# A four-layer graph kernel: the attention loop of its first layer in a written order, with a rational search step and zero rows for unused gather places

## The chip, the core and the metric

The kernel runs on one core of one Trainium2 chip. The metric is device time in microseconds (us) from the start to the end of one execution of the whole program. Five engines take part, each working through its own queue in order: TensorE (PE in the profile; its weight loads are PEld), VectorE (DVE), ScalarE (ACT), GpSimd (POOL) and SyncE (SP), which issues most DMA transfers. GpSimd issues the indirect ones, the gathers.

## What is computed

There are 4096 nodes with 256 features, one sparse 4096x4096 matrix `adj` (about 0.1% filled, and a diagonal), and four layers, each adding its output to `x` after a layer norm and a relu. Layer 0 is the expensive one. Cut to what matters:

```python
# layer 0, on h = relu(layernorm(x)); S = adj
R = S + eye;  R = R / R.sum(-1)
Xf = Xa = h;  Z = 0
for n in range(2):
    q = Xa @ W1.T @ W2.T;  k = Xa @ W3.T
    probs = softmax(q @ k.T)                  # 4096 x 4096
    # keep, in each row, the largest probabilities until 0.9 is reached
    A = probs * mask;  A = A / A.sum(-1)
    Xf = R @ Xf;  Xa = A @ Xa
    Z = Z + Xf @ U1[n].T + Xa @ U2[n].T
x = x + layernorm(h + Z) * ln_g + ln_b
# layer 1: tanh(R @ (h @ W) + b)      layer 2: graph attention with 4 heads
# layer 3: relu(adj @ (h @ W))
```

## The kernel before

**Two versions in one program.** `fast_layers` computes all four layers and counts rows in which one of its assumptions failed; only if that count isn't zero does `general_layers` compute everything again, with an exact search. In the profiled execution the fast version alone ran.

**Layer 0** is the function `layer0_step(n, ...)`, called for n = 0 and n = 1 and called step 0 and step 1 below. Each goes over 32 blocks of 128 rows. Before the loop it computes keys and queries and a guess of each row's largest logit (`minus_guess`). For a block b it then does this:

- `front(b)`: TensorE multiplies queries and keys (`pl`, L1008), ScalarE takes the exponentials into the 128x4096 tile `e` (L1011). Then comes a search for the threshold `t` below which a tenth of each row's sum lies. It has four rounds, two over the first 1024 columns and two over all 4096. In a round ScalarE passes over `e` twice with the current `t` as a bias, once with Sign and once with Relu (L1030); the pass writes a tile that nobody reads (`unread`), and its sum over the row is what counts. VectorE makes a new threshold of the two sums in a chain of operations on 128x1 columns (L1034 to L1054). In that chain GpSimd raises a ratio to a power (L1052). After the fourth round VectorE sets `hi`, an upper bound for the threshold (L1063, L1067).
- `diffuse(b)`: the product with the adjacency. In step 0 it is a full one: four transfers of 512 KB (`adj`), 33 matrix products into `pr` (L767), and VectorE marks which columns are used (`marks`, L1077, four reductions of 128x1024), and takes the reciprocal of the row sums (`rdeg`, L1080). In step 1 the used columns are known: GpSimd gathers up to 640 rows of the adjacency (`ac`) and of the values (`vg`) in five gathers each (L844), VectorE sets unused places of `ac` to zero (L1088), `ac` is written out for the later layers (L1094), and seven products follow (L859, L863). ScalarE scales the result (`xf`, L1099).
- `select(b)`: VectorE finds the exact threshold. One pass keeps what is below `hi` (`near`, L1110), 16 maxima of eight over it (`best`, L1115) and a list of the 48 largest (L1120, L1122) give the last kept value; a pass sets everything below it to zero in `e` (L1147), another removes surplus ties (L1150).
- `attend(b)`: 32 transposes on TensorE (`pat`, L1179), eight copies on ScalarE (`at`, L1181), 32 matrix products into `pa` (L1184), and a scaling (`xa`, L1186).
- `close(b)`, in step 1 only: transposes, eight products with the update weights (`pz`, L1198), a layer norm and the residual. The last four operations run on GpSimd (L737, L1215 to L1217).

**What sets the order.** The program is written for the tile framework. Its scheduler decides the order of each engine's queue from the order in the source, from its own estimate of durations, and from when buffers come free. The loop calls `front` two blocks ahead (`FRONTS = 2`, four buffers of `e`), so that the scheduler can fill one block's chain with another block's work.

**Between and after.** `list_columns` turns the marks of step 0 into lists of at most 160 columns for each quarter of the columns, cut into five index vectors of 128 (`column` for tables of values, `adj_row` for the adjacency). Unused places point at the first row of their quarter. Layers 1 to 3 use `ac` and these lists, with five gathers for each block.

Of the kernel before, what the change touches and what calls it, by code (L numbers as in the profile page):

```python
# [53 lines left out]
F32 = mybir.dt.float32  # L55
BF16 = mybir.dt.bfloat16
# [6 lines left out]
AX = mybir.AxisListType  # L63
PSUM = bass.MemoryType.PSUM
DRAM = bass.MemoryType.DRAM

P = 128
N = 4096
# [18 lines left out]
FRONTS = 2  # L87
# [558 lines left out]
def fast_layers(  # L646
# [47 lines left out]
    nc.gpsimd.memset(ones, 1.0)  # L694
    eights = const.tile([P, 8], F32, name="eights")
# [6 lines left out]
    for n in range(2):  # L702
        names = ("z", "t", "hi", "room", "full", "last", "extra")
        ends.append({k: const.tile([P, NB], F32, name=f"end_{k}{n}") for k in names})
# [6 lines left out]
    used = const.tile([P, CHUNKS, NB], F32, name="used")  # L711
# [5 lines left out]
    xf1_d = dram.tile([N, D], F32, name="xf1_d")  # L717
    xa1_d = dram.tile([N, D], F32, name="xa1_d")
    x1_d = dram.tile([N, D], F32, name="x1_d")
    q_d = dram.tile([P, N], F32, name="q_d")  # L720
    adjc_d = dram.tile([NB, P, CHUNKS + 1, P], F32, name="adjc_d")
    adj_rows = adjt.rearrange("b p c i -> (b p c) i")
# [54 lines left out]
    def list_columns(marks):  # L777

        with ExitStack() as st:
# [38 lines left out]
            nc.vector.tensor_scalar(used, at, 0.0, None, op0=ALU.is_gt)  # L818
            first = sb.tile([P, 1], F32, name="first")
            for q in range(QUARTERS):  # L820
                nc.vector.memset(first[q * 32 : (q + 1) * 32], q * float(N // QUARTERS))
            nc.vector.tensor_scalar(at, at, -1.0, 0.0, op0=ALU.add, op1=ALU.max)
            nc.vector.tensor_scalar(at, at, first, None, op0=ALU.add)
            nc.vector.tensor_copy(column, at)

            chunk_i = sb.tile([P, CHUNKS, NB], U32, name="chunk_i")
            nc.vector.tensor_scalar(chunk_i, column, 7, None, op0=ALU.logical_shift_right)
# [39 lines left out]
    def layer0_step(n, va, marks=None):  # L867

        with ExitStack() as st:
# [4 lines left out]
            tops = kt_pool.tile([P, NB, 1 + LIST], F32, name="tops")  # L874
            nc.gpsimd.memset(tops[:, :, 0:1], 0.0)
            end = ends[n]
# [86 lines left out]

            e_pool = st.enter_context(tc.tile_pool(name=f"e{n}", bufs=FRONTS + 2))
            adj_pool = st.enter_context(tc.tile_pool(name=f"adj{n}", bufs=3))
            sm = st.enter_context(tc.tile_pool(name=f"sm{n}", bufs=6))
# [5 lines left out]
            unread = one.tile([P, N], U8, name="unread")  # L972

            def small(name, width=1):
                return sm.tile([P, width], F32, name=name)

            def secant(power, old, new):

                diff, total = small("diff", 2), small("total", 2)
                for k in range(2):  # L980
# [551 lines left out]
```

## Time and profile before

| | |
|---|---|
| three runs | 4719.48, 4753.93, 4756.27 us; median 4753.93 us |
| the profiled execution | 4763.97 us, its span 4762.1 us |
| busy | PE 75%, DVE 59%, ACT 46%, POOL 28% of the span |
| up to the first logits of step 0 | 194 us |
| loop of step 0 | 194 to 1580 us |
| column lists, and what precedes the loop of step 1 | 1580 to 1787 us |
| loop of step 1 | 1787 to 3352 us |
| layers 1, 2, 3 | 390, 683 and 337 us |

The boundaries were read from the first and last instructions of each part. The share of busy time is an average over parts with different limits, so the loops are looked at one by one. A row of instruction groups gives the total busy time, the mean of one instruction in ns, and the idle time of the engine just before. In a line of the waits, the columns are the total in us, how often, and the longest. "granted clock" is the share of TensorE's full clock that it was allowed to run at.

### The profile page before, as it was taken

Reading aid. Unit: us, or ns where it says so; the run is one execution under the profiler, and the core shown is the slowest. Engines: PE = TensorE matmul, PEld = TensorE weight load, DVE = VectorE, ACT = ScalarE, POOL = GpSimd, SP = SyncE. Lnnn points to the kernel's source line nnn. Section 1 sums busy time; section 2 is a strip of 40 time slices with the busy share of each in tenths; the row PEclk is TensorE's granted clock in tenths of the full one; section 3 lists DMA queues with packets and bytes.
Section 4 is the critical chain, followed back from the end, with each engine's and each line's share of the span. In section 5 each row is a group of like instructions: output and inputs, shape, how many; then the busy total and the mean of one; then the engine's idle time right before and its main releaser. Section 6 shows DMA issues by size and latency. Waiting matters only on the chain.

```text
span 4762.1 us, 46890 instructions
## 1 busy us (share of the span) xinstructions
PE 3551.9 (75%) x14666; PEld 2659.7 (56%) x14666; DVE 2825.9 (59%) x9228; ACT 2188.1 (46%) x3157; POOL 1337.1 (28%) x1214
## 2 busy tenths in 40 slices
PE   4989899999999395878777878787455467777454
PEld 2566677677777253555555555555334356666333
DVE  2287887877888515676767676776211356666300
ACT  3377776666765016666666666664310320000300
POOL 0000010010010102444444444431046233231065
PEclk9799999999999677888888888898567765555767
DMA  2011121111112200111111111110235222221155
GB/s 74 28 55 57 53 62 56 48 61 62 53 51 65 72 26 29 42 37 44 37 44 36 45 36 45 35 32 14 85 101 165 92 80 65 68 67 39 66 166 160
DMA packets 160741, 292.11 MB, mean 61 GB/s; under 512 B 26466, under 2 KB 102626, under 8 KB 160482
## 3 DMA queue, kind: packets, MB, share of 16 engines
q1 hardware_dynamic: 124642, 193.94, 12.7%
q0 software_dynamic: 35840, 95.08, 6.7%
q8 instruction: 118, 1.93, 0.2%
q14 instruction: 141, 1.16, 0.1%
HBM read 242.65 MB, written 46.27 MB: 61 GB/s over the span
## 4 chain that ended last, share of the span: by engine, by line
DVE 27%; PE 24%; POOL 15%; issue 12%; ACT 11%; another core or an unknown queue 6%; DMA 3%; SPq 0%; DVEq 0%; POOLq 0%; ACTq 0%
ACT unread L1030 7%; POOL ratio L1052 6%; PE pa L1184 6%; PE acc L1424 5%; POOL vg L844 5%; DVE u L1410 3%; PE pv L1290 3%; DVE e L1147 2%; POOL ac L844 2%; DVE e L1150 2%; DVE best L1115 2%; PE acc L859 2%; DVE near L1110 2%; DMA ac<-in_adjt,adj_row 2%
## 5 line engine op out<-in xcount | busy, mean ns | idle before, releaser
L1030 ACT ACTIVATE unread<-e,t 128x4096 uint8<-128x4096 f32 (+1 forms) x384 | 1095.7, 2853 | 595.7 <-DVE t L1054 207.5
L1184 PE MATMUL pa<-xa,at 128*128 128x256 f32 x2048 | 619.5, 465 | 310.3 <-ACT at L1181 310.3
L1184 PEld LDWEIGHTS pa<-xa,at 128*128 128x128 f32 x2048 | 469.4, 236 | 479.4 <-ACT at L1181 395.7
L1052 POOL TENSOR_TENSOR ratio<-ratio,power 128x1 f32<-128x1 f32 x192 | 265.3, 1382 | 1086.1 <-DVE ratio L1048 610.8
L1184 PE MATMUL pa<-h,at 128*128 128x256 f32 x2048 | 509.8, 402 | 75.4 <-ACT at L1181 75.4
L1184 PEld LDWEIGHTS pa<-h,at 128*128 128x128 f32 x2048 | 395.8, 199 | 219.9 <-ACT at L1181 162.9
L767 PE MATMUL pr<-h,adj 128*128 128x257 f32 x2048 | 470.8, 384 | 13.4 <-ACT xf L1099 13.4
L1424 PE MATMUL acc<-tabg,u 128*128 128x65 f32 x1536 | 366.1, 418 | 145.4 <-DVE u L1418 139.1
L767 PEld LDWEIGHTS pr<-h,adj 128*128 128x128 f32 x2048 | 383.8, 191 | 103.5 <-issue 28.1
L1008 PE MATMUL pl<-kt,qb 64*128 64x512 f32 x1024 | 411.5, 665 | 39.5 <-ACT e L1011 39.5
L1424 PEld LDWEIGHTS acc<-tabg,u 128*128 128x128 f32 x1536 | 343.4, 329 | 173.8 <-DVE u L1418 161.4
L859 PE MATMUL acc<-vg,ac 128*128 128x256 f32 x768 | 240.4, 475 | 229.4 <-issue 77.9
L1181 ACT COPY at<-pat 128x512 f32<-128x512 f32 x512 | 284.0, 576 | 246.9 <-PE pat L1179 238.6
L844 POOL DMA_INDIRECT vg<-v_d,column x320 | 304.4, 951 | 315.1 <-DMA v_d<-v 167.2
L1115 DVE MAX8 best<-near 128x8 f32<-128x256 f32 x1024 | 372.7, 411 | 0.0
L844 POOL DMA_INDIRECT vg<-xf_d,column x160 | 268.6, 1679 | 307.5 <-PE pt L748 206.7
L859 PEld LDWEIGHTS acc<-vg,ac 128*128 128x128 f32 x768 | 178.5, 240 | 287.6 <-issue 85.4
L1011 ACT ACTIVATE e<-pl,minus_guess 128x1024 f32<-128x1024 f32 x256 | 284.2, 1117 | 117.1 <-DVE minus_guess L960 98.4
L1179 PE MATMUL pat<-ident,e 128*128 128x128 f32 x2048 | 276.3, 276 | 39.5 <-issue 24.8
L844 POOL DMA_INDIRECT tabg<-table_d,column x160 | 183.0, 1144 | 399.6 <-DVE rden L1432 269.3
L1179 PEld LDWEIGHTS pat<-ident,e 128*128 128x128 f32 x2048 | 241.5, 143 | 92.3 <-issue 55.4
L1110 DVE SCALAR_TENSOR_TENSOR near<-e,end_hi 128x4096 f32<-128x4096 f32 x64 | 286.9, 4483 | 1.0 <-DVE end_hi L1067 0.2
(486 smaller groups left out, 5205.0 us busy)
## 6 DMA issues: line engine op xcount, KB each, us to landing
adj<-in_adjt SPq DMA_DIRECT2D x128, 512.0 KB
ac<-adjc_d SPq DMA_DIRECT2D x96, 384.0 KB
adjc_d<-ac SPq DMA_DIRECT2D x32, 384.0 KB
v_d<-v SPq DMA_DIRECT2D x64, 128.0 KB
vg<-v_d SPq DMA_DIRECT2D x64, 128.0 KB
vg<-v_d,column POOLq DMA_INDIRECT x320
table_d<-tab SPq DMA_DIRECT2D x32, 132.0 KB
tabg<-table_d SPq DMA_DIRECT2D x32, 132.0 KB
```

The lines of the kernel that those rows point to most:

```text
L767: nc.tensor.matmul(acc, parts[c // CA][:, c % CA, :], v[:, c, :], start=(c == 0), stop=(c == NB - 1 and own is None),)
L844: nc.gpsimd.indirect_dma_start(out, None, rows, bass.IndirectOffsetOnAxis(ap=index, axis=0))
L859: nc.tensor.matmul(acc, ac[:, k, :], v[:, k, :], start=(k == 0), stop=(k == CHUNKS and not own))
L1008: nc.tensor.matmul(pl[:, r, :], qb[half], kt[half, j * 512 : (j + 1) * 512], start=True, stop=True)
L1011: nc.scalar.activation(e[:, j * 1024 : (j + 1) * 1024], pl.rearrange("p r c -> p (r c)"), AF.Exp, bias=minus_guess[:, b : b + 1], accum_ou ...
L1030: nc.scalar.activation(unread[:, :width], e[:, :width], func, bias=t, scale=-1.0, accum_out=to)
L1052: nc.gpsimd.tensor_tensor(ratio, ratio, power, op=ALU.pow)
L1110: nc.vector.scalar_tensor_tensor(near, e, hi, e, op0=ALU.is_lt, op1=ALU.mult, accum_out=low)
L1115: nc.vector.max(best[:, k, :], near[:, k * (N // SEG) : (k + 1) * (N // SEG)])
L1179: nc.tensor.transpose(pt[:, k, :], a[:, c * P : (c + 1) * P], ident)
L1184: nc.tensor.matmul(acc, at[:, k, :], va[:, c, :D], start=(c == 0), stop=(c == NB - 1))
L1424: nc.tensor.matmul(acc[:, h, :], u[:, k, h, :], tab[:, k, h * (DK + 1) : (h + 1) * (DK + 1)], start=(k == 0), stop=(k == CHUNKS),)
```

## The change

The change touches `fast_layers` alone.

1. The loop of `layer0_step` is cut into small functions, and `period(b)` writes out their order. It works on four blocks at a time: block b+2 gets its logits, exponentials and the two short rounds, b+1 the two long rounds and the bound, b is selected, and b-1 attended and closed. `tc.manual_schedule` makes VectorE, ScalarE and TensorE issue in just this order. The queues of GpSimd and SyncE stay the scheduler's.
2. In the search, `t * ratio ** power` gives way to a rational expression, computed on VectorE alone (`update`, `stepped`, and `bound` for the last round). A round has more column operations, and nothing on GpSimd.
3. Unused places in `column` now point at an added row N of each table, which holds zeros; so the multiplication of `ac` by `used` is dropped.
4. Smaller moves: h is stored (`h0_d`) and read back by block instead of computed again from x; the own rows of xf1 are read once more (`fb`); mean and variance of step 1 are taken in another way (`summed`, `spread`, `finish`), with the subtraction now on GpSimd; a GpSimd copy (`eighth`) takes the place of a VectorE reduction; four transposed pieces go through two copies instead of four; `adj` has four buffers in step 0 (before three), `ac` and `vg` two each in step 1 (before three).

```diff
+            def evaluate(b, k, funcs=(AF.Sign, AF.Relu)):
+                s = state[b]
+                width = PART if k < 2 else N
...
+                for func in funcs:
+                    nc.scalar.activation(
+                        unread[:, :width], s["e"][:, :width], func,
+                        bias=s["at"], scale=-1.0,
+                        accum_out=s["signs"] if func == AF.Sign else s["gap"],
+                    )
+            def measured(b, k):
...
+                nc.vector.tensor_scalar(twice, s["signs"], float(width), s["at"], op0=ALU.add, op1=ALU.mult)
+                nc.vector.scalar_tensor_tensor(
+                    low, twice, 0.5, s["gap"], op0=ALU.mult, op1=ALU.subtract
+                )
+                nc.vector.scalar_tensor_tensor(
+                    steep, s["gap"], -0.33 / 0.465, twice, op0=ALU.mult, op1=ALU.add
+                )
+                return low, steep, goal
+            def stepped(to, m, t):
+                den = small("den")
+                nc.vector.tensor_scalar(den, m, 0.5, 0.1, op0=ALU.add, op1=ALU.max)
+                nc.vector.tensor_scalar_min(den, den, 0.925)
+                nc.vector.reciprocal(den, den)
+                nc.vector.scalar_tensor_tensor(to, den, -1.0, t, op0=ALU.add, op1=ALU.mult)
+            def update(b, k):
...
+                low, steep, goal = measured(b, k)
+                den, num = small("step_den"), small("step_num")
+                nc.vector.scalar_tensor_tensor(den, low, goal, steep, op0=ALU.add, op1=ALU.mult)
+                nc.vector.scalar_tensor_tensor(num, low, goal, s["gap"], op0=ALU.subtract, op1=ALU.mult)
+                nc.vector.reciprocal(den, den)
+                m = small("m")
+                nc.vector.scalar_tensor_tensor(m, num, 0.5 / 0.465, den, op0=ALU.mult, op1=ALU.mult)
+                pair = small("next_pair", 2, 8)
+                stepped(pair[:, 0:1], m, s["at"])
...
-                    nc.gpsimd.tensor_tensor(ratio, ratio, power, op=ALU.pow)
...
+            def load(b):
+                s = state[b]
+                if n == 0:
+                    s["adj"] = load_adj(adj_pool, b)
+                    return
+                ac = s["ac"] = adj_pool.tile([P, CHUNKS + 1, P], F32, name="ac")
+                nc.sync.dma_start(ac[:, CHUNKS, :], adjt[b, :, b, :])
+                for k in range(CHUNKS):
+                    gather(ac[:, k, :], adj_rows, adj_row[:, k, b : b + 1])
+                nc.sync.dma_start(adjc_d[b], ac)
+                s["vg"] = gathered(adj_pool, xf1_d, b)
...
+            def diffused(b):
+                s = state[b]
+                if n == 0:
+                    nc.vector.reciprocal(rdeg[:, b : b + 1], s["pr"][:, D : D + 1])
+                s["xf"] = wk.tile([P, D], F32, name="xf", bufs=3)
+                nc.scalar.mul(s["xf"], s["pr"][:, :D], rdeg[:, b : b + 1])
...
+            def period(b):
+                old, cur, mid, new = (0 <= k < NB for k in (b - 1, b, b + 1, b + 2))
+                if n == 1 and 0 <= b - 2:
+                    finish(b - 2)
+                if cur:
+                    load(b)
+                if new:
+                    logits(b + 2, 0)
+                if mid:
+                    evaluate(b + 1, 2, (AF.Sign,))
+                if cur:
+                    below(b)
+                if n == 1 and cur:
+                    diffuse(b)
+                    diffused(b)
+                if old:
+                    flip(b - 1, 0)
+                    flip(b - 1, 1)
+                    take(b - 1, (0, 1))
+                    if n == 0:
+                        diffused(b - 1)
+                if mid:
+                    evaluate(b + 1, 2, (AF.Relu,))
+                    update(b + 1, 2)
+                if new:
+                    exponentials(b + 2)
+                if old:
+                    attend(b - 1, 0)
+                    attend(b - 1, 1)
+                    flip(b - 1, 2)
+                    flip(b - 1, 3)
+                    take(b - 1, (2, 3))
+                if new:
+                    logits(b + 2, 1)
+                    exponentials(b + 2)
+                    evaluate(b + 2, 0)
+                if cur:
+                    listing(b)
+                    if n == 0:
+                        mark(b, (0, 1))
+                if new:
+                    aim(b + 2)
+                    update(b + 2, 0)
+                if old:
+                    attend(b - 1, 2)
+                    attend(b - 1, 3)
+                    flip(b - 1, 4)
+                    flip(b - 1, 5)
+                    take(b - 1, (4, 5))
+                if mid:
+                    evaluate(b + 1, 3, (AF.Sign,))
+                if old:
+                    attend(b - 1, 4)
+                    attend(b - 1, 5)
+                    flip(b - 1, 6)
+                    flip(b - 1, 7)
+                    take(b - 1, (6, 7))
+                if mid:
+                    evaluate(b + 1, 3, (AF.Relu,))
+                if cur:
+                    decide(b)
+                    cut(b)
+                if mid:
+                    bound(b + 1)
+                if old:
+                    attend(b - 1, 6)
+                    attend(b - 1, 7)
+                    attended(b - 1)
+                    if n == 1:
+                        own_rows(b - 1)
+                        turn(b - 1, 0, state[b - 1]["fb"], va[:, b - 1, :D])
+                        turned(b - 1, 0)
+                if n == 0 and cur:
+                    diffuse(b)
+                    mark(b, (2, 3))
+                if new:
+                    evaluate(b + 2, 1)
+                    update(b + 2, 1)
+                if cur:
+                    drop(b)
+                if n == 1 and old:
+                    turn(b - 1, 1, state[b - 1]["xf"], state[b - 1]["xa"])
+                    turned(b - 1, 1)
+                    combine(b - 1)
+                    summed(b - 1)
+                    spread(b - 1)
+            with tc.manual_schedule(engines={ENGINES.DVE, ENGINES.Activation, ENGINES.PE}):
+                for b in range(-2, NB + 2 if n == 1 else NB + 1):
+                    period(b)
```

The new names stand for old work: `logits` is L1008, `exponentials` L1011, `evaluate` one round's Sign and Relu passes (rounds k = 0 to 3), `below` is L1110 and the 16 maxima, `listing` L1120 and L1122, `decide` L1126 to L1143, `cut` L1147, `drop` L1150 and the three operations after it, `flip` and `take` the transposes and copies of `attend`, each for 512 columns (group g of eight), `turn`, `turned` and `combine` the same for `close`. `bound` has 32 column operations, `update` 11 (12 for k = 2).

## The prediction

> **What bounds the kernel now.** I read the stages first: the share of busy time, stretch by stretch (us, then busy time and count of PE, PEld, DVE, ACT, POOL, then granted clock, DMA share, GB/s).
>
> ```profile
> 194.00:1580.00 1386.00, 1272.39 (x5696) 967.27 (x5696) 1109.34 (x3702) 935.81 (x1089) 120.64 (x132) 0.97 0.18 56
> 1787.00:3352.00 1565.00, 1193.67 (x4792) 861.02 (x4792) 1060.03 (x3787) 994.11 (x1311) 667.43 (x547) 0.87 0.12 38
> ```
>
> In step 0 TensorE is nearly full; in step 1 no engine is, so waits set the pace. `near` (L1110) starts at 234.9 and last at 1525.4 in step 0, at 1830.1 and 3293.0 in step 1: 41.6 and 47.2 us a block. Then the waits:
>
> ```profile
> POOL ratio L1052 <- DVE ratio L1048: 641.3, 89, 16.4
> ACT unread L1030 <- DVE t L1054: 207.5, 88, 11.6
> ACT unread L1030 <- DVE end_z L1019: 194.2, 28, 7.6
> ACT xf L1099 <- DVE rdeg L1080: 26.9, 17, 2.1
> ```
>
> ScalarE waits for thresholds that pass through GpSimd. The last line, small now, matters below: only a reciprocal of `pr` stands before `xf`. The trace in order of time shows why GpSimd is slow, and what a dependent VectorE operation costs:
>
> ```profile
> 854.35 0.25 DVE L1132 TENSOR_SCALAR out__6135<-ahead_of,end_room 128x48 f32<-128x48 f32 x1
> 854.63 0.21 DVE L1134 SCALAR_TENSOR_TENSOR kept<-out__6135,tops 128x48 f32<-128x48 f32 x1
> 854.87 0.20 DVE L1136 TENSOR_REDUCE end_t<-kept 128x1 f32<-128x48 f32 x1
> ...
> 2306.92 4.49 DVE L1110 SCALAR_TENSOR_TENSOR near<-e,end_hi 128x4096 f32<-128x4096 f32 x1
> ...
> 2307.03 4.78 POOL L1052 TENSOR_TENSOR ratio<-ratio,power 128x1 f32<-128x1 f32 x1 [1.48 <-DVE power L1045]
> ```
>
> A power beside `near` lasts 4.78 us, otherwise 0.55. Each of the first three operations starts 0.03 us after its predecessor ends. The large groups (busy total, mean ns, idle before):
>
> ```profile
> L1030 ACT ACTIVATE unread<-e,t 128x4096 uint8<-128x4096 f32 x256 | 948.8, 3706 | 290.1 <-DVE t L1054 153.2 <-DVE ra L1153 95.2 <-issue 30.6
> L1147 DVE SCALAR_TENSOR_TENSOR e<-e,end_t 128x4096 f32<-128x4096 f32 x64 | 286.6, 4477 | 0.0
> L1150 DVE MATCH_REPLACE8 e<-drop,e 128x4096 f32<-128x4096 f32 x64 | 282.2, 4409 | 0.0
> ```
>
> TensorE's pieces, run together:
>
> ```profile
> 801.50 3.73 PE L1184 MATMUL pa<-h,at 128*128 128x256 f32 x16
> 805.06 1.03 PE L1179 MATMUL pat<-ident,e 128*128 128x128 f32 x8
> 819.33 14.18 PE L767 MATMUL pr<-h,adj 128*128 128x257 f32 x64
> ```
>
> **The change, part by part.** VectorE, per block: `below` 4.52 and 16 maxima starting 0.327 apart, 9.8; `listing`, five rounds of 0.717 and a last maximum, 3.9; `decide` 1.8; `cut` 4.5; `drop` 4.4 and three columns, 4.9; marks 4 x 1.13. The column operations last 0.145 to 0.21 (L1034 to L1067), and in a written chain each waits for the last: `update`, 11, is 1.8 by that spacing, `bound`, 32, 4.8. The nearest extremes are 0.07 each, if all ran independently (0.8 and 2.2), and 0.24 (2.6 and 7.7). I take 1.8 and 4.8, since nearly all are dependent. With `aim` 0.3, VectorE needs 40 in step 0, 36 in step 1 (no marks, `summed` 0.6).
>
> *Step 0.* Let `below(b)` start at 0. ScalarE did the long Sign pass during the preceding `drop`, copies two pieces by 4, and next in its queue is `xf(b-1)`. Its `rdeg` stands behind `below(b)` in VectorE's queue, although `pr` is ready: 9.95. That is a new wait of 6, and behind it on ScalarE are the long Relu pass and everything after. Adding ScalarE's rows: `xf` to 10.3, Relu 3.8 to 14.1, two exponentials at 1.10, two copies 0.95, two exponentials to 19.4, two short passes at 1.24 to 21.8, two copies to 22.8, Sign 3.7, copies 1.2 with a short wait to 27.7, Relu to 31.5. `bound(b+1)` on VectorE waits for that (it was free at 30.0): to 36.3; marks 2.3, `update` 1.75, `drop` 4.9: 45.2. VectorE has waited 4.15 + 1.4.
>
> TensorE is done with the first two groups at 8.2; its next item, the second half of the logits, waits for `pl`, which the exponentials free at 15.3: idle for 7.2. What such a gap costs shows in stretches of 3.4 us (granted clock third from the end):
>
> ```profile
> 2149.10:2152.50 3.40, 0.06 (x1) 0.00 (x0) 0.56 (x2) 3.40 (x3) 2.20 (x4) 1.00 0.07 19
> 2152.50:2155.90 3.40, 2.42 (x6) 1.95 (x7) 1.67 (x11) 3.40 (x7) 2.91 (x4) 0.51 0.24 66
> 2155.90:2159.30 3.40, 3.40 (x10) 2.64 (x9) 1.23 (x8) 1.89 (x5) 2.44 (x3) 0.50 0.31 93
> 2159.30:2162.70 3.40, 3.40 (x17) 2.28 (x16) 1.11 (x5) 2.13 (x4) 0.56 (x1) 0.99 0.10 33
> ```
>
> One empty stretch, then 6.8 at half clock: up to 3.4 us lost, and 0 if the slow part falls into the gap. The groups that follow (3.7 of products, 1.0 of transposes) are on the path, since ScalarE's copies wait for them with no slack. Most of the slow part falls after the gap, so I take 2.5: 47.7 a block, 6.1 more than now. Times 31: +189.
>
> The Trainium skill ("TensorE: Matmul & The Clock Gate", Part 1) says that half rate ends after one busy window of about 3.4 us. By that alone the loss would be 1.7, step 0 +164 and the kernel 4670; this trace shows two windows.
>
> *Step 1.* There is no `rdeg`. ScalarE waits at 0 for `summed`, then `spread` 0.6, Sign 3.7, `xf` 0.4 (seven products, done at 3.4), copies 1, Relu 3.7, exponentials 2.2, copies 0.95, exponentials 2.2, short passes 2.4, copies 0.95, Sign 3.7, copies 1.2, Relu 3.8: 26.8. Then `bound` 4.8, `update` 1.75, `drop` 4.9, `summed` 0.6: 38.9. TensorE's gaps are under 2.8 each, so I add 0.3 for its clock: 39.2 against 47.2, times 31: -248.
>
> *At nothing:* the removed powers (265.3 us of L1052) and L1088 (0.83 x 32, on VectorE's path before) are inside these sums. `eighth` on GpSimd, between 0.15 and 4.8 with a wait like the power's, is needed only at the end. The subtraction on GpSimd (between 0.35, L741 on VectorE, and 1.4) hides beside VectorE's maxima; uncovered it costs only the tail. `h0_d`, 4 MB, is about 19 by the wait for x at the start, hidden by what precedes the loop. SyncE gets two more 128 KB reads a block; behind its write of `ac`, which waits for the gathers, stand `qb` and these, all with two buffers, so a block early. The gathers' number is unchanged; some 160 of 640 places are unused (128 rows at 0.1% hit about 480 columns) and now read one row instead of four: between 0 and +32 (TensorE's 31.6 us of waits for gathers in layers 1 and 3, doubled); I take 0. Filling and draining the loops stays at about 40 and 55 us: 0, +-15.
>
> **Sum:** 4764.0 + 189 - 248 = 4705 against the profiled execution; the median of the runs is 10 lower: 4695.
>
> **The rivals.** *Step 0 stays warm:* if the slow clock falls into the gap, 45.2 a block, +112: 4620. For it: the gap is twice the empty stretch. Against: the slow part above lasted 6.8.
>
> *The scheduler still places `rdeg` early,* so that the written order isn't what the queue gets, or the columns overlap more: step 0 at VectorE's 40 to 41.6: 4460 to 4510. For it: the wait was at most 2.1 us before. Against: `rdeg` is on an ordered engine.
>
> *Slower: gathers late in step 1.* `diffuse(b)` now stands ahead of block b-1's transposes in TensorE's queue, and these feed the whole ScalarE chain. Slack is 0.9; each us beyond costs 32. The kernel gets slower than now by 1% from 4.2 us on. If GpSimd issues block b's gathers in its own period, after `finish` (at 8) and at 1.25 each, they end at 20.5, 17 late: 5210. For it: one queue in order, two buffers instead of three, and GpSimd waited 206.7 us for a buffer of `vg`. Against: that buffer is now freed by `diffuse(b-2)`, so the gathers can run a period ahead. A few us late: 4850.
>
> *The rational step misses,* and `general_layers` runs: 28 passes like L1110 for 64 blocks alone are 8030 us. Against: both forms share goal and bounds.
>
> **How the numbers follow.** Forecast 0.50, between 4640 and 4760; warm clock 0.17; early `rdeg` 0.10; late gathers 0.20; miss 0.03. The range 4530 to 4850 leaves out half of the early case and most of the late ones. About 1% (48 us) is what a measurement of this kernel can tell from no change; below 4706 lie 0.29 of the forecast and the two gains, 0.56; within 1% 0.21 and 0.02 of late gathers, 0.23; slower 0.21.
>
> **What would show it.** In step 0: `near` 47.7 apart (13 or 14 of the stretches), "ACT xf <- DVE rdeg" the largest new wait at about 6 x 31 us, TensorE idle 7 us before the second logits and half clock after it. In step 1: `near` 39.2 apart, VectorE over 90% busy, no wait of `pr` for gathers. I am wrong if step 0 gets faster, or if step 1 gains less than 5 us a block.

## The result, and the profile after

The changed kernel took 4902.6 us in the median (four runs, 4883 to 4921) against 4755.1 for the kernel before, run beside it: a ratio of 1.033, 95% interval 1.027 to 1.040. It is slower by 3%; 4695 was forecast. The profiled execution took 4921.4 us, its span 4919.2. Here and below a time is the median of all runs, and a ratio compares only those in the faster of two states that the runs of a kernel show.

First the two loops, as in the first view of before: one stretch for each, us, then busy time and count of PE, PEld, DVE, ACT, POOL, granted clock, DMA share, GB/s.

```profile
235.00:1704.00 1469.00, 1194.00 (x5390) 923.98 (x5391) 1175.24 (x3792) 893.06 (x1028) 6.45 (x31) 0.89 0.16 51
2007.00:3454.00 1447.00, 1061.40 (x4494) 795.14 (x4495) 1058.94 (x3756) 930.34 (x1149) 507.95 (x466) 0.85 0.15 44
```

Step 0 was near the forecast and step 1 was not: `near` starts 47.4 us apart in step 0 (41.6 before, 47.7 forecast) and 46.7 in step 1 (47.2 before, 39.2 forecast). In the steady part both loops have the same period, 47.78 us, which is 14 of the 3.41 us stretches of the clock. Everything outside the two loops kept its length.

The waits, in us in total, times, and the longest:

```profile
DVE next_pair L1068 <- ACT unread L1038: 286.7, 61, 7.0
...
PE pr L872 <- DVE h L1346: 144.6, 30, 6.6
...
ACT xf L1304 <- DVE full_goal L1089: 138.6, 21, 6.6
...
ACT at L1249 <- remote: 133.6, 28, 5.4
...
ACT xf L1304 <- DVE rdeg L1302: 69.2, 10, 8.6
```

GpSimd's wait for a ratio (641.3 us before) is gone. The two lines of `xf` together, 208 us in 31 blocks, are the forecast wait for `rdeg` (a small operation that starts at the same time is sometimes named in its place). The line "at <- remote" was not forecast: ScalarE waits 4.8 us in each of 28 blocks, and no operation of another engine ends when that wait ends ("remote": the profile names no operation that ended it).

One period of step 0, in order of time, with the wait before each in brackets:

```profile
895.95 4.48 DVE L1156 SCALAR_TENSOR_TENSOR near<-e,end_hi 128x4096 f32<-128x4096 f32 x1
...
898.30 1.07 ACT L1249 COPY at<-pat 128x512 f32<-128x512 f32 x2 [3.27 <-PE pat L1242]
...
905.78 0.15 DVE L1302 RECIPROCAL rdeg<-pr 128x1 f32<-128x1 f32 x1
905.96 0.47 ACT L1304 ACTIVATE xf<-pr,rdeg 128x256 f32<-128x256 f32 x1 [6.59 <-DVE rdeg L1302]
906.34 3.70 ACT L1038 ACTIVATE unread<-e,next_pair 128x4096 uint8<-128x4096 f32 x1
...
910.16 0.16 DVE L1068 SCALAR_TENSOR_TENSOR pair<-twice,gap 128x1 f32<-128x1 f32 x1 [4.05 <-ACT unread L1038]
...
911.27 3.78 PE L1010 MATMUL pl<-kt,qb 64*128 64x512 f32 x8 [7.73 <-ACT e L1022]
914.98 4.53 PE L1258 MATMUL pa<-h,at 128*128 128x256 f32 x16
```

This is the forecast chain: the reciprocal starts 9.8 us after `near`, because it stands behind the maxima; `xf` waits 6.6 for it; the long pass and VectorE's update follow late; and TensorE, idle for 7.7, runs its next pieces at half clock (it has gone cold, as it is called below).

The same view of one period of step 1, where `near` started at 2796.80:

```profile
2813.68 1.04 PE L1242 MATMUL pat<-ident,e 128*128 128x128 f32 x8
...
2814.39 0.19 ACT L1038 ACTIVATION_READ_ACCUMULATOR unread<-e,ones 128x1 f32 x1
...
2816.46 0.96 POOL L857 DMA_INDIRECT vg<-xf_d,column  x1 [0.30 <-issue]
...
2819.31 1.07 ACT L1249 COPY at<-pat 128x512 f32<-128x512 f32 x2 [4.73 <-remote]
...
2819.95 4.63 PE L1258 MATMUL pa<-xa,at 128*128 128x256 f32 x10 [5.23 <-ACT at L1249]
```

The eight transposes end at 2814.7 and ScalarE is free from 2814.6, but its copy of them starts at 2819.3. An engine tells the others by a signal (the update of a semaphore) that an operation is done. The trace's records of signals show what ScalarE waited for: TensorE's signal for these transposes arrives at 2819.29, 4.6 us after their end. In between GpSimd is sending off the last of ten gathers. TensorE stands idle for 5.2 us by then and goes on at half clock.

### The profile page after: what moved, and what is told of

Its sections match the earlier page's. It is cut to its first block, busy times and chain, and to the rows that moved or that the text cites. A ratio compares the mean times of both kernels' runs of the same rounds, so it can differ in the third digit from the quotient of the medians.

```text
span 4919.2 us, 47246 instructions
## 1 busy us (share of the span) xinstructions
PE 3462.0 (70%) x14666; PEld 2645.9 (54%) x14666; DVE 2970.5 (60%) x9617; ACT 2176.2 (44%) x3061; POOL 1081.9 (22%) x1057
## 5 line engine op out<-in xcount | busy, mean ns | idle before, releaser
L1038 ACT ACTIVATE unread<-e,next_pair 128x4096 uint8<-128x4096 f32 (+1 forms) x384 | 1097.2, 2857 | 226.6 <-DVE next_pair L1082 220.5
L1258 PE MATMUL pa<-xa,at 128*128 128x256 f32 x2048 | 542.4, 424 | 165.5 <-ACT at L1249 165.5
L1258 PEld LDWEIGHTS pa<-xa,at 128*128 128x128 f32 x2048 | 426.1, 214 | 275.9 <-ACT at L1249 209.4
L1010 PE MATMUL pl<-kt,qb 64*128 64x512 f32 x1024 | 329.9, 765 | 333.4 <-ACT e L1022 315.4
L775 PE MATMUL pr<-h,adj 128*128 128x257 f32 x2048 | 450.5, 379 | 0.0
L1010 PEld LDWEIGHTS pl<-kt,qb 64*128 64x128 f32 x1024 | 105.3, 224 | 471.1 <-ACT e L1022 360.6
L1162 POOL COPY eighth<-best 128x16 f32<-128x16 f32 x64 | 13.5, 211 | 1545.3 <-DVE full_goal L1089 1068.2
L1161 DVE MAX8 best<-near 128x8 f32<-128x256 f32 x1024 | 340.9, 411 | 6.3
L1365 POOL TENSOR_TENSOR scale<-var,minus_half 128x1 f32<-128x1 f32 x32 | 143.2, 4474 | 853.7 <-DVE var L1363 853.7
L1202 DVE SCALAR_TENSOR_TENSOR e<-e,end_t 128x4096 f32<-128x4096 f32 x64 | 286.6, 4478 | 0.0
```

Source lines behind the costliest of these rows:

```text
L775: nc.tensor.matmul(acc, parts[c // CA][:, c % CA, :], v[:, c, :], start=(c == 0), stop=(c == NB - 1 and own is None),)
L1010: nc.tensor.matmul(pl[:, r, :], s["qb"][rows], kt[rows, j * 512 : (j + 1) * 512], start=True, stop=True,)
L1038: nc.scalar.activation(unread[:, :width], s["e"][:, :width], func, bias=s["at"], scale=-1.0, accum_out=s["signs"] if func == AF.Sign else ...
L1161: nc.vector.max(best[:, k, :], near[:, k * (N // SEG) : (k + 1) * (N // SEG)])
L1202: nc.vector.scalar_tensor_tensor(s["e"], s["e"], last, s["e"], op0=ALU.is_ge, op1=ALU.mult, accum_out=s["held"])
L1258: nc.tensor.matmul(s["pa"], s["at", g][:, k, :], va[:, c, :D], start=(c == 0), stop=(c == NB - 1))
```

## The experiments

I held four theories. A: step 0 is slow because `xf` on ScalarE waits for `rdeg`, which stands behind `below` on VectorE. B: ten gathers in one go hold back TensorE's signals in step 1. C (added after the first runs): whether signals are late depends on the chip or the run, and not on the code. D: what is left above 39.2 in step 1 is TensorE's slow clock after its wait for `summed`. A last group takes the change apart. The runs came on five occasions, each on another chip, with the kernel before beside them on the same chip; ratios are to that.

**The reciprocal moved.**

```
                     take(b - 1, (0, 1))
-                    if n == 0:
-                        diffused(b - 1)
...
                     take(b - 1, (4, 5))
+                    if n == 0:
+                        diffused(b - 1)
```

> After's kernel with one move in step 0: the reciprocal of the row sums and the scaling of block b-1 (diffused) come behind the copies of pieces 4 and 5, not behind those of 0 and 1. Theory A (step 0 is 47.8 us a block because ScalarE waits for a reciprocal that stands behind `below` on VectorE): the waits of xf for rdeg, full_goal and the like in step 0 (234 us) go, near starts 42 to 43 us apart there instead of 47.4, the kernel is 130 to 170 us shorter, about 4750. Rival (TensorE's slow clock after its gap locks step 0 to 14 stretches of 3.41 us, whatever ScalarE waits for): under 40 us, above 4860.

4512.6 us, ratio 0.965 (0.960 to 0.970). Step 0:

```profile
240.00:1564.00 1324.00, 1164.41 (x5383) 919.26 (x5384) 1175.09 (x3791) 882.38 (x1028) 6.42 (x31) 0.95 0.18 56
```

Its VectorE does the same 1175 us of work, in 1324 us and not in 1469, at a granted clock of 0.95 and not 0.89: 42.7 us a block. Theory A holds: the place of the reciprocal, and of the scaling that waits for it (both were moved), costs 145 us. But the kernel gained more than that, because step 1, whose code is as in after, ran at 40.5 us a block. Three other kernels ran on the same chip:

**Fewer gathers, or later ones.**

```
-            gather(v[:, k, :], v_d, column[:, k, b : b + 1])
+            nc.sync.dma_start(v[:, k, :], v_d[k * P : (k + 1) * P, :])      (vg plain, step 1's loop)
...
-                    gather(ac[:, k, :], adj_rows, adj_row[:, k, b : b + 1])
+                    nc.sync.dma_start(ac[:, k, :], adjt[b, :, k, :])        (ac plain)
...
                     below(b)
+                if n == 1 and 0 <= b - 2:
+                    finish(b - 2)                                            (finish behind below)
```

> After's kernel, but in the loop of step 1 the rows vg are read by five plain reads of fixed rows on SyncE's queue instead of five gathers on GpSimd's (so the diffusion there adds the wrong rows; the same bytes). Theory B (ten gathers in one go hold back the signals that TensorE sends, 4.6 us for the copies of pieces 4 and 5, and TensorE goes cold by it): the 133.6 us of ScalarE's remote waits go, near is 40 to 42 us apart in step 1 instead of 46.7, the kernel about 4700 to 4750. Rival B2 (the five gathers of adjacency rows, or the write of the 384 KB of ac, hold the signal): the remote waits stay near 4.7 us a block and the time within 40 us of 4902. Rival B3 (the signal was only the first of several waits of the same length, so another takes its place, the slow clock above all): the remote waits go and the time falls by less than 60 us.

> After's kernel, but in the loop of step 1 the adjacency rows ac are read by five plain reads of fixed chunks on SyncE's queue instead of five gathers (so the diffusion there multiplies wrong weights; the same bytes). The gathers of vg then run from 8 to 14.5 us after near instead of from 14.5 to 20.6. Theory B (ten in one go hold the signal): the remote waits go or shrink under 2 us a block, 4700 to 4760. If five gathers of 1 KB rows are enough to hold a signal, it is held earlier in the period, at the copies of pieces 2 and 3, and the time stays above 4830.

> After's kernel with finish(b-2) emitted behind below(b): VectorE starts near without the wait for the spread on ScalarE (0.73 and 0.15 us a block), and on GpSimd the ten gathers of block b come ahead of finish(b-2), so about 6 us later in the period before or at its start. Theory B: the held signal moves with the gathers to another hand-over, between 4 us a block worse and, if it falls into ScalarE's long passes, 5 us a block better: 4700 to 5030, with the late deliveries ending where the gathers end. Rival (the hold belongs to pieces 4 and 5 or to the write of ac, not to the gathers): late deliveries stay at the copies of pieces 4 and 5, and the time falls by 25 to 30 us for the wait on the spread alone.

4656.3, 4653.7 and 4642.3 us, ratios 0.993 (0.989 to 0.996), 0.995 (0.992 to 0.999) and 0.992 (0.989 to 0.995). Step 1 had 40.5 us a block in all three and none of the waits "remote". Taken alone the two kernels with plain reads would have looked like a proof of theory B. They are none: the kernel with the moved reciprocal kept all ten gathers and had 40.5 too.

**After and before once more.** So after was run with nothing changed on another chip, and before on two.

> After's kernel with nothing changed, run once more, since the four runs above all showed step 1 at 41.0 us a block, the one in which step 1's code is the same as after's too. Theory C (late signals of TensorE during gathers depend on the chip or the run, and step 1 of after is 41.0 us a block wherever they are on time): either late deliveries are counted in hundreds and step 1 is near 46.7, ratio 1.033, or there are a handful and step 1 is near 40.5, between the loops 285 to 288 us and not 303, ratio 0.992 to 0.998. Rival (the code of step 0 decides by the phase in which step 1 is entered): few late deliveries, but step 1 at 46.7 all the same.

> The kernel before with nothing changed, for its profile where signals of TensorE come on time (or not). If late signals cost it something too, its step 0 and step 1 stay near 41.6 and 47.2 us a block, and the 72 us by which it was faster there (4683 and 4687 against 4755) lie between the loops and in the layers behind them. If step 1 too was slowed by them, it shows below 46.

> The kernel before, for its profile. On a chip with signals on time: the 70 us by which it is faster there than on the others lie between the loops (some 15, as for after) and behind the loops (40 to 95, as for after), and its two loops stay at 1290 and 1464 us. If its second loop is shorter by more than 30 us, late signals cost before something in step 1 as well.

After took 4656.0 us there, ratio 0.994 (0.991 to 0.998), with this in its two loops:

```profile
236.00:1704.00 1468.00, 1195.20 (x5389) 926.01 (x5390) 1174.67 (x3789) 892.79 (x1028) 6.41 (x31) 0.89 0.16 51
1992.00:3249.00 1257.00, 1007.29 (x4494) 757.26 (x4495) 1061.83 (x3755) 926.57 (x1149) 505.96 (x466) 0.91 0.17 51
```

Step 0 is the same to a microsecond; step 1 is 190 us shorter with the same operations on every engine. The place shown above, in this run:

```profile
2533.56 1.04 PE L1242 MATMUL pat<-ident,e 128*128 128x128 f32 x8
...
2534.27 0.19 ACT L1038 ACTIVATION_READ_ACCUMULATOR unread<-e,ones 128x1 f32 x1
2534.36 1.05 ACT L1249 COPY at<-pat 128x512 f32<-128x512 f32 x2
...
2534.98 3.72 PE L1258 MATMUL pa<-xa,at 128*128 128x256 f32 x16 [0.38 <-ACT at L1249]
```

The copy starts as soon as ScalarE is free, and TensorE stays warm. I counted as late TensorE's signals that arrive over 0.6 us after the modelled end of the last matmul before them, and measured the parts of each profiled run from the starts of `near`:

| run | late signals | start to loop | step 0 | between | step 1 | behind |
|---|---|---|---|---|---|---|
| before, first | 175 | 234.9 | 1290.5 | 304.8 | 1462.8 | 1469.1 |
| before, third occasion | 163 | 235.3 | 1287.6 | 303.5 | 1464.1 | 1464.5 |
| before, fifth occasion | 3 | 231.8 | 1286.0 | 293.1 | 1464.9 | 1365.4 |
| after, first | 222 | 235.7 | 1468.7 | 303.3 | 1446.5 | 1465.1 |
| after, second occasion | 3 | 236.0 | 1468.5 | 287.9 | 1256.6 | 1370.3 |

Theory C holds as far as that it isn't the code alone: the same kernel has three late signals on one occasion and some 170 or more on another. All profiled runs of an occasion were of the same kind. Since each chip was used on one occasion, chip and occasion can't be told apart; "a chip with late signals" is short for both. Before has none in its loops on either kind, so both loops take the same time; nearly all its late ones lie in the sparse layers behind, which are about 100 us longer in these profiled executions. In the medians it loses some 70 (4751 and 4755 against 4682 to 4687). After loses much the same there, and 190 us more in step 1, where 56 signals are late.

**Is it the ten gathers?** Theory B could only be tested on a chip with late signals, and the chip can't be chosen.

```
-    s["vg"] = gathered(adj_pool, xf1_d, b)            (in load; load a period ahead)
...
+    held = small("held_seen")
+    nc.gpsimd.tensor_copy(held, state[b]["held"])     (waits for cut(b))
+    state[b + 1]["vg"] = gathered(adj_pool, xf1_d, b + 1)
...
+    with tc.manual_schedule(engines={..., ENGINES.Pool}):
```

> The kernel with plain reads of vg in step 1's loop once more (the diffusion there adds the wrong rows). Where after's own run beside it has late deliveries: Theory B (ten gathers in one go hold the signals) has near at 41.0 in step 1 and none late there; rival B2 (the other gathers or the write of ac) has 46.7 and about 2 late ones a block. Where after's own run has none, both are 41.0.

> After's kernel with the ten gathers of a block in two bursts of five: those of adjacency rows behind finish, those of vg behind a 128x1 copy on GpSimd that waits for what cut gives, some 10 us later; the same bytes, the same gathers, all results as before. Theory B (where a chip delivers late, it is ten gathers in one go that hold TensorE's signals, until 2.9 us after the last of them starts): no late signals in step 1's loop, its period 41 us and not 46.7, ratio 0.99 to 1.00 on a chip with late signals (counts near 170 from the sparse layers behind remain). Rival (the write of ac, or any gather at all): late ones stay, at another hand-over, and the period is above 44. On a chip with signals on time: 41.0 in any case.

> The kernel with plain reads of ac in step 1 once more (the diffusion there multiplies wrong weights), five gathers a block instead of ten. On a chip with late signals: Theory B has no late signals in step 1's loop and 41 us a block; if gathers of 1 KB rows alone are enough, late ones of up to 4 us stay and the period is above 44.

> After's kernel with the ten gathers in two bursts of five, once more. On a chip with late signals: Theory B has none late in step 1's loop and a period of 41 us; the rival (any gather, or the write of ac) has late ones at another hand-over and above 44. On a chip with signals on time 41.0 and nothing learned on this.

All four had their signals on time and 40.5 us a block (4623.0, 4626.4, 4622.5 and 4621.9 us); they decide nothing on B. What speaks for B comes from the runs on the other kind. In after all 56 late signals of step 1 arrive 2.78 to 3.03 us after the issue of the last of ten gathers. In the kernel with the power put back (below) the median of 55 is 2.81. In a kernel with finish behind below (the third of the next group) the gathers end 4 us earlier in the period, and the median of 60 late signals is again 2.90 after the last one; they are late by only 1.25 us there and cost little. Once their loops are steady, before sends at most five gathers at a time and the kernel without the written order at most six, and no signal is late there. The latter kernel begins step 1 with 15 gathers in a row, and three signals are late just behind these.

The layers behind the loops tell one rival off. In the first run of after 79 of the 222 late signals lie in layer 1, 82 in layer 3, and none in layer 2. Layers 1 and 3 gather rows of values alone, mostly in runs of 10 to 45 at a time, and write no `ac`; layer 2 gathers five at a time for most of its length, and none of its 90 signals is late. The other five runs with late signals show the same. So neither the gathers of adjacency rows nor the write of `ac` is needed for late signals, and long runs of gathers go with them. It is still a pattern and not a test: in layers 1 and 3 some signals are late behind five gathers only, 10 us after a longer run, and the two runs with the bursts taken apart met no late signals.

**Both moves, and what is left of step 1.** The first kernel has the reciprocal behind `update(b + 1, 2)`, the scaling behind the second exponentials, and finish behind below; the second also has step 1's gathers and diffusion product a period ahead, the product in TensorE's gap, and `z` in a buffer of the transposes; the third has the moves and fills that gap:

```
+                if n == 1 and cur and mid:
+                    diffuse(b + 1)                                       (second)
                 if n == 1 and old:
                     turn(b - 1, 1, ...)
...
                     logits(b + 2, 0)
+                if n == 1 and old:
+                    idle = ps.tile([P, 4, P], F32, name="pat", tag="pmisc")
+                    for k in range(28):
+                        nc.tensor.transpose(idle[:, k % 4, :], ident, ident)   (third)
```

> After's kernel with both moves: in step 0 the reciprocal on VectorE behind update(b+1, 2) and the scaling on ScalarE behind the second exponentials, where neither waits; in step 1 finish(b-2) behind below(b). If signals are on time: step 0 from 42.9 to about 41.5 us a block, as the 1.2 us that xf still waited and half of VectorE's 2.55 us go; step 1 41.0 as before; about 4470 where the kernel before is 4683, ratio 0.955. If signals are late during gathers: step 0 the same, step 1 between 41 and 47.8.

> The kernel of both moves, and in step 1 the gathers of block b+1 asked for a period ahead, its diffusion product put into TensorE's gap before the second turn of block b-1, and z in a buffer of the transposes, so that the product doesn't wait for summed. Theory D (on time, step 1 is 41.0 and not 39.2 because TensorE goes cold in the 5.5 us for which the product waits for h, and xf then waits 1.6 us for it): step 1 at 37.5 to 39.5 us a block, the kernel 50 to 110 us below the one with both moves. Rival (VectorE's own 36 us and its waits for the Relu pass set 41.0): within 20 us of the one with both moves.

> The kernel of both moves, with 28 transposes more a block in step 1 (their results are read by nobody), in the 4.8 us in which TensorE waits for summed ahead of the diffusion product. Theory D (the slow clock after that gap makes the product 5.5 us instead of 3.1, xf waits 1.5 us for it and VectorE 1.2): step 1 from 41.0 to 39.5 to 40, the kernel 30 to 45 us below the one with both moves. Rival (VectorE's chain takes it back elsewhere, as when the product was moved): within 15 us.

The kernel of both moves: 4433.6 us, ratio 0.946 (0.940 to 0.952), step 0 at 40.4 us a block, a us better than I expected and close to the 40 that VectorE's operations were summed to; step 1 unchanged at 40.5. The product moved into the gap: 4396 to 4470 us in four runs, too far apart to compare; in the profiled one, 4430.9 us, step 1 again had 40.5. Where TensorE's idle time went:

```profile
2491.16 5.49 PE L872 MATMUL pr<-vg,ac 128*128 128x256 f32 x12 [4.71 <-DVE h L1344]
```

```profile
2501.60 6.62 PE L1258 MATMUL pa<-xa,at 128*128 128x256 f32 x16 [4.75 <-ACT at L1249]
```

In the first kernel (the first line) the product comes after 4.71 us of idling and takes 5.5 instead of 3.1. In the second the product is early, but now TensorE idles 4.75 us for ScalarE's copies, and the next products take 6.6 instead of 3.7. The gap was moved and not closed, so this didn't test theory D. The third kernel closes it, as the granted clock shows (first line the third kernel, second the one of both moves, 900 us of step 1):

```profile
2100.00:3000.00 900.00, 752.41 (x3912) 580.60 (x3911) 771.26 (x2685) 664.89 (x836) 315.08 (x352) 0.99 0.18 54
```

```profile
2100.00:3000.00 900.00, 735.86 (x3293) 554.54 (x3291) 777.62 (x2681) 662.67 (x829) 281.32 (x347) 0.91 0.18 52
```

But it ran on a chip with late signals: 4486 to 4558 us in four runs, ratio 0.947 (0.937 to 0.957), step 1 at 40.7. Whether a warm TensorE is worth 1 us a block in step 1 stays open, since late signals took 1.25 us of each period there. It does show that nearly all of step 1's gain can be kept even there: 40.7 us a block where after has 46.7. Whether the moves or the filling did it was not told apart.

**The change taken apart.** The search step's power put back into the written order; the written order taken away; and both:

```
-            with tc.manual_schedule(engines={ENGINES.DVE, ENGINES.Activation, ENGINES.PE}):
+            if True:                                                     (no written order)
...
+                nc.gpsimd.tensor_tensor(ratio, ratio, power, op=ALU.pow)
+                nc.vector.tensor_mul(to, t, ratio)                       (power, in update and bound)
```

> After's kernel with the search step's power put back on GpSimd in update and bound (a ratio raised to the power, as before), the written order and all else as after. The prediction held that the removed powers are worth what the chains of columns lose: four hops a block of 0.55 and two crossings, about 1 us each, so +4 us a block in step 0 and more in step 1, where a power stands in GpSimd's queue behind ten gathers of 1.25: +150 to +450 us against after. Rival (the powers hide where the engines wait for each other): under +60.

> After's kernel without the written order: the scheduler orders VectorE, ScalarE and TensorE as it did before, the new search step and the zero rows stay. Theory A says that one placing in the written order (the reciprocal behind below) costs step 0 150 us and the rest of it brings step 1 some 200: the scheduler's order then has step 0 at 40 to 44 us a block without that wait, and step 1 above 43. Rival (the new search step alone makes the gain, the order adds nothing): step 1 at or under 41.

> After's kernel without the written order once more, as the ground for the next: ratio 0.90 to 0.93 on a chip with late signals, 0.91 to 0.95 on one without (where before itself is faster).

> The kernel without the written order, and with the search step's power back on GpSimd. Theory E (the new search step makes the gain and the written order gives it back): the time goes back most of the way, to a ratio of 0.97 to 1.01, with GpSimd's waits for ratio back at hundreds of us. Rival (the gain of the freely ordered kernel comes from the other parts: a look-ahead of four buffers, split functions, wider columns): within 60 us of the freely ordered kernel.

On a chip with late signals: with the power 4921.1 us, 1.035 (1.028 to 1.043), not to be told from after's 1.033; without the written order 4376.7 us, 0.919 (0.911 to 0.927). On one with signals on time: without the written order 4280.1 us, 0.914 (0.907 to 0.921); without it and with the power 4434.2, 0.944 (0.939 to 0.950). I missed three of the four: the power costs nothing that shows in the written order, where I expected at least 150 us; step 1 without the order is at 38, not above 43; and putting the power back returns 154 of 405 us, not most. Nor is the wait for `rdeg` gone without the order: ScalarE still idles 4.8 us for it in most blocks of step 0.

The two loops of the kernel without the written order, and what the power brings back in the last kernel:

```profile
238.00:1430.00 1192.00, 1118.54 (x5199) 875.10 (x5198) 1077.72 (x3778) 878.93 (x1012) 6.46 (x31) 0.98 0.18 60
1727.00:2904.00 1177.00, 1005.48 (x4427) 752.69 (x4428) 978.49 (x3750) 920.42 (x1130) 480.75 (x457) 0.92 0.18 53
```

```profile
POOL ratio L1090 <- DVE ratio L1089: 634.3, 94, 10.2
...
POOL ratio L1090 <- DVE by L1135: 373.7, 61, 15.1
```

Both loops are shorter than in after: 38.5 and 38.0 us a block, with TensorE 94% busy in step 0. In its order VectorE starts a column of `update` between two of the maxima, and the reciprocal 2 us after `pr` is done, where the written order runs one function to its end before the next. It beats both kernels and every version with moves, by ratio (0.914; both moves 0.946). It isn't the order of before: `period` still gives the order in the source that the scheduler starts from.

In sum, on chips with signals on time (before took 4686.7 and 4685.5 us on the two occasions used): everything but the written order and the new search step, the new order in the source included, -251 us (4685.5 to 4434.2), the new search step another -154, the written order +376 (4280 to 4656; that order with the power was not run there). The two moves take back some 220 of the 376 (4656.0 to 4433.6). What makes up the -251 was not taken apart. With late signals the written order costs more, from 0.919 to 1.033, though these two ratios come from two occasions.

## Why the prediction was wrong

**Step 0, forecast +189, measured +178: right.** `xf` at 10 us after `near`: measured 10.0. New wait of 6: 6.6. TensorE's gap 7.2: 7.7. Slow clock 2.5: the logits took 3.78 instead of 1.99 and the next products 4.53 instead of 3.73, 2.6 together. The period settled at 14 stretches, where the marker had 13 or 14.

For the slow clock the Trainium skill ("TensorE: Matmul & The Clock Gate", Part 1) has full speed back after one busy window, from which the prediction estimated a loss of 1.7. The stretches of after in the period shown (TensorE busy for 1.93, 3.45 and 3.40 us of each; granted clock third from the end):

```profile
909.80:913.20 3.40, 1.93 (x6) 0.86 (x8) 2.70 (x17) 3.40 (x8) 0.00 (x0) 0.50 0.00 0
913.20:916.65 3.45, 3.45 (x10) 1.68 (x7) 3.24 (x12) 2.83 (x6) 0.00 (x0) 0.50 0.06 19
916.65:920.05 3.40, 3.40 (x20) 3.00 (x20) 2.54 (x14) 2.09 (x5) 0.00 (x0) 1.00 0.00 0
```

TensorE starts again within a stretch, the next one it is busy throughout, and then the clock is full. So the trace agrees with the page; the 1.7 left out the broken stretch ahead of the whole one, and the prediction's reading of "two windows" in the trace of before, the first busy for 2.42 of 3.40 us, was the same thing.

**Step 1, forecast -248, measured -16: wrong, by two terms.** The large one is 190 us, the late signals. The sum let ScalarE take each group of transposes when TensorE had ended it ("Sign 3.7, copies 1.2, Relu 3.8"), so it put the wait for TensorE's signal at nothing; here the signal came 4.6 us after the end, TensorE went cold in that time, the next copies waited 2.4 more, and the loop settled at 47.8. The rival "gathers late in step 1" had the right place for the trouble, GpSimd's queue, and nearly the time, 4850; but its mechanism was a product that waits for its rows, and there is no such wait. Could it have been seen? The profile of before held 175 late signals, all outside the two loops; I had not looked for them.

The small term is the sum itself. With signals on time step 1 gains 208 (1464.9 to 1256.6), 40 less than forecast. "TensorE's gaps are under 2.8 each" was wrong: before the diffusion product it idles 4.7, because `pr` shares a buffer with `z` and waits for `summed`; so the product is slow and `xf` 0.9 later than summed up. And finish's first operation, on VectorE ahead of `near`, waits for the spread on ScalarE, 0.9 us that I took for free. Taking that away alone did not shorten the loop, though (40.5 with finish behind below): `near` came earlier, but `xf` then started 6.0 us after it and not 5.2, still waiting for the product. Closing the gap could not be read, so the cause of these 40 us stays open; they are read from the chain and not shown by a run.

**At nothing: not contradicted.** Between and behind the loops before and after differ by some 5 us at most in the table, on either kind of chip. But the part behind, whose code all versions of after share, took 1368 to 1374 us in some profiled executions with signals on time and 1402 to 1411 in others, so single executions can't show costs of less than some 40 us there for the zero row, `h0_d`, the extra reads and the subtraction on GpSimd.

**The removed powers "are inside these sums": right in a way that I had not meant.** In the written order they are worth nothing that shows (1.035 with the power, 1.033 without), presumably since something else sets the period; that was measured with late signals and the misplaced reciprocal alone. The whole change was argued as order plus step; the larger fact, that the scheduler's own order with the same parts is 8% faster than the written one, and 3% faster than the one with both moves, was in the forecast only as a rival with a chance of 0.10, for one operation of it, and at 4460 to 4510, some 100 us above what that kernel took.

## What to carry to other kernels

When an order is written by hand, look in it for small operations that free another engine and stand behind a long one: a 0.15 us reciprocal behind 9.8 us of other work cost 145 us here, and moving it, with the scaling that waits for it, showed in a single run. The wait by itself need not cost that: the kernel without the written order keeps a wait of 4.8 us for the same reciprocal and is faster all the same. Before crediting a written order with a gain, run the same parts without it: here that was the fastest kernel of all. And before reading an experiment, run the unchanged kernel beside it on the same chip, since two kernels that seemed to prove a cause only showed another occasion.

## What the runs showed of the hardware

How promptly TensorE's signals arrive while gathers are under way differed between occasions, each on another chip. On five occasions three late signals were counted in a run on four, and 163 to 227 on one (and in the first two profiles). Late ones arrive some 2.9 us after the issue of the last gather of a burst in step 1's loop, and up to 22 us after the last matmul in the sparse layers (25 in before), where several then arrive 0.04 us apart. The counts are rough: where signals are late, 129 to 208 of some 2100 have no record of their arrival, elsewhere 14 at most. The transfers themselves are hardly slower there: the 4 KB packets of step 1's gathers take 234 ns on average in the first run of after and 229 in the second. Why it happens on some occasions, no run shows.

Loops whose clock drops alike in every period were seen to settle on a whole number of clock stretches: 47.78 us is 14 of 3.413, 40.96 is 12 of them, 47.78 in both loops of after's first run, 40.96 in its step 1 wherever signals are on time. Step 1 of before, too, has 47.7 in its steady part, close to 14. Small savings may vanish inside such a period: 0.9 us a block by finish behind below moved nothing (40.95 against 40.96), though there the wait for the product explains it as well. In step 0 with the reciprocal moved the clock drops in some periods and not in others, and the periods of 42.9 and 40.5 us are no such multiples.

A 128x1 power on GpSimd took 4.74 us beside `near` in after's step 1, and 0.58 when finish came behind below, out of its way. With signals on time that move made no difference to the period (40.95 against 40.96), although the ten gathers stand behind finish in GpSimd's queue.
